# Results used one step later, and a ninth chain on GpSimd: one change to a four-stage convolutional network kernel

## The chip, the cores and the metric

The kernel is one launch on 1 core of one Trainium2 chip. The metric is the device time of that launch in microseconds, taken as the median of the runs shown. The core has five engines that each work through their own queue in order and meet only at semaphores: TensorE (PE; its weight loads are listed apart as PEld), VectorE (DVE), ScalarE (ACT), GpSimd (POOL) and SyncE (SP), which here only issues DMAs. An instruction that waits holds up everything behind it on its own engine.

## The reference, cut to what matters

Four images of 256 channels by 64 x 64 points pass through four layers, all in float32.

```python
# layer 0: 1x1 convolution, depthwise 3x3, offsets and masks; deformable sampling:
#   y = sum over 9 points of bilinear(image, grid + offset) * mask     (the gathers)
#   then the squeeze-and-excite scale and a feed-forward block
# layer 1: linear attention
#   qkv = relu(bn(w x));  agg = relu(pointwise(depthwise5x5(qkv)))     (the chains)
#   vk  = sum over points of v k^T;  out = (vk q) / (ksum q + eps);  x + relu(bn(w out))
# layer 2: 3x3 convolution with binarised weights, plus x
# layer 3: pooled attention: softmax(theta(x)^T phi(pool(x))) g(pool(x)), plus x
```

## The kernel before, in words

**Stages.** Images are handled one behind the other. `sample(n)` gathers image n (L554 to L674) while earlier images go through the later layers beside it. When the fourth image is gathered, the tail begins: `feedforward(3)`, then `layer1(3)` beside what is left of `layer2(2)` and `layer3(2)`, then `layer2(3)` beside the last rows of `layer3(2)`, then `layer3(3)` alone.

**How work is laid side by side.** Every layer is a generator. `beside` (L1183) advances the main one by a step, then advances each of the others until the costs they yielded reach their share. Inside `with ordered()` the instructions of PE, DVE, ACT and POOL stand in their queues exactly in the order in which the generators issue them; SP's order is left to a scheduler. So a `yield` is where other work may come in between, and whether it does depends on the costs. One round below is one step of `sample`: four gathers (`gathered`, L587) and eight matmuls on what they brought. Two rounds share a half of the PSUM tile `acc`, which ACT copies out at L603; after seven rounds the gather buffers `g` are used up, and a gather waits for PE.

**`layer3`, rows** (L1125 to L1158). For each of 32 rows of an image: two matmuls into `s`, DVE's maxima `mx` (L1138), ACT's exponentials `pe` (L1143), twice four transposes by PE (L1149) with a copy by ACT into `pT` (L1150), eight matmuls (L1154), DVE's reciprocal `rden` (L1156) and ACT's scaling into `m2` (L1157). A copy comes directly behind its transposes; L1154, L1156 and L1157 are issued without a yield between them.

**`layer1`.** `rows` makes 48 tiles of q, k and v (L805 to L815) into padded images `pad0` and `pad1`. Each of 24 chains is a depthwise 5 x 5 convolution of one padded image: on DVE it is 25 instructions over 1024 elements (taps, L178 and L180, in `depthwise`) that add up in the PSUM tile `agg`. In the tail (`alone` is true) every third chain goes aside: `products` (L186) makes 25 products on ACT (L193) and 24 additions on POOL (L194), one for every second tap of the two DVE chains beside it, and the next three chains begin when all are done. Everything else of the layer waits in the list `later`, from which `step` takes one item: `both` (transposes, the copy L853 and sums), `dens` (a matmul, DVE's L895 and the reciprocal L896), four times `head` (matmul L903, scaling L905) and twice `proj` (matmuls L911, ACT's L913, DVE's addition L914) for each half of an output block. In the tail a tap in two takes an item; what is left when the taps are done is worked off by L975.

**PSUM.** Eight banks: `agg` two, `acc`, `dp` and `vk` one each, and three under the tag `mm`, which all other results take in turn through `ps`. In the tail, the convolution's long sums take `acc` and `dp` instead.

Of the kernel before, what the change touches and what calls it, by code (L numbers as in the profile page):

```python
# [17 lines left out]
P = 128  # L18
# [23 lines left out]
LINEAR, LAST = 930, 620  # L42
# [29 lines left out]
class Net:  # L72
    def __init__(self, ctx, tc, a, out):
        self.tc, self.nc, self.a, self.out, self.kept = tc, tc.nc, a, out, []
        e = ctx.enter_context
        self.cp = e(tc.tile_pool(name="const", bufs=1, side="left"))
        self.ps1 = e(tc.tile_pool(name="ps1", bufs=1, space=PSUM))
        self.mm = e(tc.tile_pool(name="mm", bufs=3, space=PSUM))
        self.banks, self.alone = cycle(["mm"]), False
        self.dp = e(tc.tile_pool(name="scratch", bufs=1, space=DRAM))  # L80
# [105 lines left out]
    def products(self, pool, acc, src, w, k, rows, cols, r0, bias, step):  # L186

        nc = self.nc
        for t in range(k * k):
            s = src[:, r0 + t // k:r0 + t // k + rows, t % k:t % k + cols]  # L190
            if t:
                m = pool.tile([P, rows, cols], F32, name="m", tag="product", bufs=3)
                nc.scalar.activation(m, s, AF.Copy, scale=w[:, t:t + 1])  # L193
                nc.gpsimd.tensor_tensor(acc, acc, m, ALU.add)  # L194
            else:
                nc.scalar.activation(acc, s, AF.Identity, bias=bias, scale=w[:, t:t + 1])
# [551 lines left out]
    def layer1(self, n, st, st2):  # L748
# [3 lines left out]
        with tc.tile_pool(name=f"la{n}", bufs=1, side="right") as sp, \  # L752
# [14 lines left out]
            later, count, aside = [], 0, None  # L767
            room = lambda bufs, more=1: bufs + more * self.alone

            def step(cost, chains=False):  # L770


                nonlocal count
                count += chains
                if later and (not self.alone or count % 2 or not chains):
                    later.pop(0)()
                if chains:
                    if count % 8 == 6 if self.alone else count in LEADS:
                        next(made, None)
                    if count % 2 and aside:  # L780
                        next(aside, None)
                return cost

# [4 lines left out]
            def rows():  # L790


                for t, tiles in enumerate(((2, 4), (3, 5), (0, 1))):
                    new = lambda c: [self.padded(bp, 1, 20, 2, c, f"pad{i}", bufs=room(3, 2)) for i in range(2)]
                    pads = {0: new(0)}
                    for b in range(NB):
# [5 lines left out]
                        for i, m in enumerate(tiles):  # L802
                            ps = self.ps()
                            for k in range(KT):
                                nc.tensor.matmul(ps, qw[:, k, m * P:(m + 1) * P], x[:, k], start=k == 0, stop=k == KT - 1)  # L805
                            bn = {"bias": qb[:, m:m + 1], "scale": self.vec("qkv_s", m)}
# [14 lines left out]
                            yield  # L821
# [20 lines left out]
            def outer(t, kind, kv, vv, first, last):  # L842

                at = [slice(i, i + 256) for i in range(0, kv.shape[1], 256)]
                kts = []

                def turned(cs):
                    pt = self.ps("pt").rearrange("p (s j c) -> p s j c", s=2, j=2)
                    for j in range(2):
                        nc.tensor.transpose(pt[:, 0, j], kv[:, cs][:, j * P:(j + 1) * P], self.ident)  # L850
                        nc.tensor.transpose(pt[:, 1, j], vv[:, cs][:, j * P:(j + 1) * P], self.ident)
                    kts.append(bp.tile([P, 2, 2, P], F32, name="kt", tag="kt", bufs=4))
                    nc.scalar.copy(kts[-1], pt)  # L853
# [7 lines left out]
                def both(i):  # L861
                    if i < len(at):
                        turned(at[i])
                    if i:
                        added(i - 1)

                later.extend(partial(both, i) for i in range(len(at) + 1))
# [15 lines left out]
            def output(c, qp, aq):  # L883
# [3 lines left out]
                rd, xv, ot = [], [], {}  # L887

                def dens():
                    pd = self.ps("den")  # L890
                    for h in range(2):
                        for j in range(4):
                            nc.tensor.matmul(pd[32 * j:32 * j + 32], ld[:, j, h], qh[h][j], start=h == 0, stop=h == 1)
                    rd.append(bp.tile([P, 512], F32, name="rd", tag="v1"))
                    nc.vector.tensor_scalar(rd[0], pd, EPS_ATT, None, ALU.add)  # L895
                    nc.vector.reciprocal(rd[0], rd[0])  # L896

                def head(h, j):
                    if not j:
                        xv.append(self.block(bp, self.x3_d[n], 2 * c + h, "xq", bufs=1))  # L900
                    hs, i = slice(64 * (j // 2), 64 * (j // 2) + 64), 2 * h + j % 2
                    pb = self.ps("rden")
                    nc.tensor.matmul(pb, self.con("sel")[hs, i * P:(i + 1) * P], rd[0][hs], start=True, stop=True)  # L903
                    ot[h, j] = bp.tile([P, 512], F32, name="ot", tag="kt", bufs=4)
                    nc.vector.tensor_tensor(rw(ot[h, j]), qh[h][j], rw(pb), ALU.mult)  # L905

                def proj(h, m):
                    b, x = 2 * c + h, xv[h]
                    ps = self.ps()
                    for j in range(4):  # L910
                        nc.tensor.matmul(ps, pw[:, j, m * P:(m + 1) * P], ot[h, j], start=j == 0, stop=j == 3)  # L911
                    r = bp.tile([P, 512], F32, name="pr", tag="v0")
                    nc.scalar.activation(r, ps, AF.Relu, bias=self.vec("proj_b", m), scale=self.vec("proj_s", m))  # L913
                    nc.vector.tensor_tensor(x[:, m], x[:, m], r, ALU.add)  # L914
# [4 lines left out]
                later.append(dens)  # L919
                for h in range(2):  # L920
                    later.extend([partial(head, h, j) for j in range(4)] + [partial(proj, h, m) for m in range(KT)])
# [25 lines left out]
            if self.alone:  # L947
                for _ in range(8):
                    next(made)
                    yield step(1)  # L950
# [7 lines left out]

            while number < 6 * NCH:
                count = 0 if not self.alone and number % 2 == 0 else count  # L960
                *args, more = yield from chain()
                if self.alone:

                    *slow, smore = yield from chain()
                    aside = products(*slow, **smore)
                    yield from aggregate(*args, **more)
                    *args, more = yield from chain()
                    yield from aggregate(*args, **more)
# [363 lines left out]
```

## Time and profile before

| what | value |
|---|---|
| median of 3 runs | 7762.42 us (7758.1 to 7763.21) |
| the profiled execution | 7748.26 us, its span 7746.5 us |
| granted TensorE clock, mean | 0.839 |
| PE busy | 5899.6 us, 76% |
| DVE busy | 5126.8 us, 66% |
| POOL busy | 5035.0 us, 65% |
| ACT busy | 2148.7 us, 28% |
| gathers | first at 133.2 us, last at 6283.4 us |

Busy times are sums over the whole span. They do not tell which engine sets the pace of a stage, so the stages have to be looked at one by one. A row of a group of instructions reads: line, engine, operation, output and inputs, shapes and count, then busy time and mean duration in ns, then how long the engine stood idle directly before such instructions and what ended that. A row of the waits reads: waiting engine, its instruction, who released it, then the sum in us, the count and the longest.

### The profile page before, as it was taken

The page shows a single profiled execution, that of the slowest core. Times are in us where ns is not written, and L with a number is a line of the kernel's source. Part 1 is how long each engine was busy: PE and PEld are TensorE (multiplying, and loading weights), DVE is VectorE, ACT ScalarE, POOL GpSimd, SP SyncE. Part 2 cuts the span into 40 slices and gives each one's busy share as a digit, 9 for nine tenths or more (in the row PEclk, how much of TensorE's full clock was granted, in tenths as well). Part 3 has the DMA queues.
Part 4 walks back from the last instruction along what each step waited for, and adds up shares of the span by engine and source line. Part 5 has one row for each costly group of instructions (what it writes and reads, how often), then busy time and mean ns, then how long its engine had stood idle before and what let it go on. Part 6 is the DMA issues. An engine that isn't in the chain of part 4 may idle for free. (4 is left out here: it accounts for less than half of the span.)

```text
span 7746.5 us, 94023 instructions
## 1 busy us (share of the span) xinstructions
PE 5899.6 (76%) x35776; PEld 3468.2 (45%) x35776; DVE 5126.8 (66%) x6429; ACT 2148.7 (28%) x4623; POOL 5035.0 (65%) x4870
## 2 busy tenths in 40 slices
PE   5666666579676677888767778988677779977899
PEld 2333333334333333446545433466454434744487
DVE  6555553644788887239888883289888843999623
ACT  1111111112222211222233222222332222656415
POOL 2777777777777777767777667777776630866210
PEclk7676776779777677999888888999888889988999
DMA  6564664555544444555544445465444442211221
GB/s 188 152 178 137 171 173 140 164 182 157 159 123 124 128 139 135 167 151 160 150 137 132 118 149 161 139 171 159 137 132 123 120 132 65 75 52 36 76 81 52
DMA packets 744338, 1031.38 MB, mean 133 GB/s; under 512 B 354128, under 2 KB 459984, under 8 KB 742352
## 3 DMA queue, kind: packets, MB, share of 16 engines
q0 software_dynamic: 221184, 604.27, 27.0%
q1 hardware_dynamic: 522704, 421.10, 18.3%
q8 instruction: 283, 4.64, 0.3%
q14 instruction: 167, 1.37, 0.1%
HBM read 856.39 MB, written 168.61 MB: 132 GB/s over the span
## 5 line engine op out<-in xcount | busy, mean ns | idle before, releaser
L591 POOL DMA_INDIRECT g<-tab,sl x4608 | 4502.1, 977 | 1781.0 <-issue 1267.5
L178 DVE SCALAR_TENSOR_TENSOR agg<-pad,vec,agg 128x1024 f32<-128x1024 f32 x2280 | 2933.9, 1287 | 61.8
L598 PE MATMUL acc<-g,wm 128*32 128x128 f32 x18432 | 1288.4, 322 | 1248.4 <-ACT at L603 711.4
L598 PEld LDWEIGHTS acc<-g,wm 128*32 128x32 f32 x18432 | 631.2, 122 | 1955.1 <-ACT at L603 941.0
L1037 PE MATMUL ps<-xd,w 128*128 128x256 f32 x3072 | 711.4, 384 | 8.2 <-DVE x L1017 2.8
L582 DVE TENSOR_TENSOR wm<-con,sl 128x768 f32<-128x768 f32 x384 | 365.5, 953 | 412.6 <-PE acc L598 396.9
L1037 PEld LDWEIGHTS ps<-xd,w 128*128 128x128 f32 x3072 | 576.8, 192 | 108.2 <-issue 29.6
L618 ACT COPY dT<-dp 64x128 f32<-64x128 f32 x1152 | 295.7, 257 | 1117.2 <-PE dp L608 794.3
L730 PE MATMUL ps<-x2f,f 128*128 128x512 f32 x1024 | 479.1, 616 | 4.0 <-ACT f L705 4.0
L805 PE MATMUL ps<-xr,qw 128*128 128x512 f32 x768 | 454.4, 723 | 15.7 <-DVE ot L905 7.7
L740 PE MATMUL ps<-hm,f 128*128 128x512 f32 x1024 | 462.0, 600 | 0.0
L715 DVE SCALAR_TENSOR_TENSOR hm<-ps,vec,lk 128x512 f32<-128x512 f32 x256 | 192.1, 750 | 399.9 <-ACT lk L732 395.9
L988 POOL TENSOR_TENSOR xd<-xp 128x640 f32<-128x640 f32 x64 | 79.4, 1269 | 472.9 <-ACT xp L1000 280.9
L603 ACT COPY at<-acc 128x256 f32<-128x256 f32 x576 | 214.1, 372 | 488.6 <-PE acc L598 474.3
L732 ACT ACTIVATE lk<-ps,low 128x512 f32<-128x512 f32 x256 | 175.9, 687 | 595.5 <-PE ps L730 595.5
L608 PE MATMUL dp<-ident,at 128*128 128x128 f32 x1152 | 272.3, 324 | 73.2 <-ACT dT L618 61.2
L631 PE MATMUL po<-dT,ow 128*128 128x288 f32 x1024 | 307.6, 449 | 13.6 <-ACT dT L626 6.5
L1154 PEld LDWEIGHTS ps<-gt,pT 128*128 128x128 f32 x2048 | 289.6, 222 | 62.1 <-issue 40.3
L1154 PE MATMUL ps<-gt,pT 128*128 128x129 f32 x2048 | 303.6, 310 | 7.3 <-ACT pT L1150 6.9
L194 POOL TENSOR_TENSOR ak<-ak,m 128x1024 f32<-128x1024 f32 x96 | 227.2, 2366 | 114.1 <-ACT m L193 109.8
L730 PEld LDWEIGHTS ps<-x2f,f 128*128 128x128 f32 x1024 | 191.5, 195 | 230.0 <-issue 217.3
L1137 PE MATMUL s<-ph,th 128*128 128x512 f32 x512 | 274.2, 649 | 22.8 <-DVE r L1164 6.3
(243 smaller groups left out, 7395.8 us busy)
## 6 DMA issues: line engine op xcount, KB each, us to landing
g<-tab,sl POOLq DMA_INDIRECT x4608
x<-x SPq DMA_DIRECT2D x128, 512.0 KB
xr<-x SPq DMA_DIRECT2D x96, 512.0 KB
tab<-xo SPq DMA_DIRECT2D x192, 128.0 KB
x<-in_x SPq DMA_DIRECT2D x32, 512.0 KB
y<-yc SPq DMA_DIRECT2D x32, 512.0 KB
yb<-y SPq DMA_DIRECT2D x64, 256.0 KB
x<-yb SPq DMA_DIRECT2D x64, 256.0 KB
```

What stands on the lines that cost most here:

```text
L178: nc.vector.scalar_tensor_tensor(to, s, wt, acc, ALU.mult, ALU.add)
L582: nc.vector.tensor_tensor(wm, self.con("own").unsqueeze(1).unsqueeze(1).to_broadcast(sh), blocks[b][:, r:r + WR, G:].unsqueeze(3).to_broad ...
L591: nc.gpsimd.indirect_dma_start(out=g[:, i, :], out_offset=None, in_=table, in_offset=bass.IndirectOffsetOnAxis(ap=sl.bitcast(I32)[:, r, i: ...
L598: nc.tensor.matmul(acc[32 * i:32 * i + 32, :], wm[:, r4, 4 * i + 2 * x:4 * i + 2 * x + 2, :], g[:, i, x * P:(x + 1) * P], start=x == 0, st ...
L618: nc.scalar.copy(dT[b][hs, :, r:r + UR], dp[u][hs, :, :, s, :].rearrange("p v g o -> p g v o"))
L631: nc.tensor.matmul(po[m][:, 0:BR * OB], self.ow[:, k, m * P:(m + 1) * P], dT[b][:, k].rearrange("p r o -> p (r o)"), start=k == 0, stop=k ...
L730: nc.tensor.matmul(ps, f1[:, k, m * P:(m + 1) * P], x2[:, k], start=k == 0, stop=k == KT - 1)
L740: nc.tensor.matmul(ps, f2[:, k, m * P:(m + 1) * P], hm[:, k], start=k == 0, stop=k == 4 * KT - 1)
L805: nc.tensor.matmul(ps, qw[:, k, m * P:(m + 1) * P], x[:, k], start=k == 0, stop=k == KT - 1)
L1037: nc.tensor.matmul(ps[:, e], w[:, k, t, 2 * half + e, m * P:(m + 1) * P], v[:, 2 * half + e, k, t:t + 8], start=i % 6 == 0, stop=i % 6 == 5)
L1137: nc.tensor.matmul(s[i], tv[:, 4 * b + j], ph[:, i * 512:(i + 1) * 512], start=True, stop=True)
L1154: nc.tensor.matmul(ps[:, 0:P + 1], pT[:, m], gt[:, m], start=m == 0, stop=m == 7)
```

## The change

1. **`layer3`**: a yield stands between the four transposes and their copy, between the eight matmuls and `rden`, and between `rden` and `m2`. The costs of a row still add up to 9.5. While `spare` is set (the ordered part of the tail), `s` of the third image's rows goes to `acc` and `dp` instead of `mm`.
2. **`layer1` beside sampling**: the addition L914, with the statistics and the store that follow it, is issued an item later than its ACT instruction. `dens` and its reciprocal, and a head's matmul and its scaling, stay together.
3. **`layer1` in the tail**: every item is cut into stages (`staged`), and a stage is issued an item behind the one before. An output block is now 18 items instead of 13, with its heads and projections reordered; a key-value product of 256 points takes one item more. Half of the `rden` matmuls use the bank `vk`.
4. **The aside in the tail**: nine chains instead of eight, taken one after another from the same sequence and advanced by a fixed fraction at every tap, not in groups of three. POOL's addition is issued a step behind ACT's product. 15 chains stay on DVE.
5. **Buffers in the tail**: `kt`/`ot` 4 to 6, the projection's `xq` 1 to 2, `pad0` and `pad1` 5 to 4 each, the convolution's `xp` 1 to 2. A matmul of `rows` is one step ahead of its ACT instruction. The convolution's additions come three matmuls later. The cost of the layer is set to 592 from 620, that of a drained item to 2 from 4.

```diff
-LINEAR, LAST = 930, 620
+LINEAR, LAST, ASIDE = 930, 592, 9
...
     def products(self, pool, acc, src, w, k, rows, cols, r0, bias, step):
...
+        made = []
+        for t in range(k * k + 3):
+            if t < k * k:
+                s = src[:, r0 + t // k:r0 + t // k + rows, t % k:t % k + cols]
+                m = pool.tile([P, rows, cols], F32, name="m", tag="product", bufs=3) if t else acc
+                made.append(m)
+                if t:
+                    nc.scalar.activation(m, s, AF.Copy, scale=w[:, t:t + 1])
+                else:
+                    nc.scalar.activation(m, s, AF.Identity, bias=bias, scale=w[:, t:t + 1])
+            if 2 <= t <= k * k:
+                nc.gpsimd.tensor_tensor(acc, acc, made[t - 1], ALU.add)
             yield step(0.5)
...
-                    if count % 2 and aside:
-                        next(aside, None)
+                    if aside:
+                        due += ASIDE * 28 / (6 * NCH - ASIDE) / 25
+                        while due > 1:
+                            next(aside, None)
+                            due -= 1
...
+            def staged(items):
+                for i in range(len(items) + max(map(len, items)) - 1):
+                    now = [it[i - k] for k, it in enumerate(items) if 0 <= i - k < len(it)]
+                    later.append(lambda now=now: [f() for f in now])
...
+                if alone:
+                    staged([(partial(turned, cs), partial(copied, i), partial(added, i)) for i, cs in enumerate(at)])
...
+                if alone:
+                    order = [heads[0, j] for j in range(4)] + [heads[1, 0], outs[0, 0], heads[1, 1], outs[0, 1], heads[1, 2], heads[1, 3]]
+                    staged([(dens, inverse), none, none] + order + [none, outs[1, 0], outs[1, 1]])
+                else:
+                    joined = lambda *fs: [f() for f in fs]
+                    items = [(partial(joined, dens, inverse),)]
+                    for h in range(2):
+                        items += [(partial(joined, *heads[h, j]),) for j in range(4)]
+                        items += [(partial(joined, *outs[h, m][:2]), outs[h, m][2]) for m in range(KT)]
+                    staged(items)
...
+            def others():
+                for _ in range(ASIDE):
+                    while not (args := next(every)):
+                        yield
+                    *args, more = args
+                    yield from products(*args, **more)
...
             while later:
-                yield step(4)
+                yield step(2 if alone else 4)
...
-                    if not wide:
+                    if not wide and not self.spare:
                         s = [self.ps("s") for _ in range(2)]
...
                             nc.tensor.transpose(pt[:, m], pe[:, (4 * i + m) * P:(4 * i + m + 1) * P], self.ident)
+                        yield 1
                         nc.scalar.copy(pT[:, 4 * i:4 * i + 4], pt)
-                    yield 3
+                    yield 1
                     ps = self.ps()
                     for m in range(8):
                         nc.tensor.matmul(ps[:, 0:P + 1], pT[:, m], gt[:, m], start=m == 0, stop=m == 7)
+                    yield 1.5
                     rden = bp.tile([P, 1], F32, name="rden")
                     nc.vector.reciprocal(rden, ps[:, P:P + 1])
+                    yield 1.5
                     nc.scalar.activation(m2[:, j * P:(j + 1) * P], ps[:, 0:P], AF.Copy, scale=rden)
-                    yield 3
```

## The prediction, made before the changed kernel was run

> **What bounds the kernel now.** I read the windows first, to get the engines stage by stage, then the waits inside the stages that are not full, then a stretch of the timeline to see one wait pass through the queues.
>
> From 133 to 6283 us POOL gathers. Rows of the timeline show the pace: 0.95 us for a gather and 0.30 us of issue, 1.25 us in all, 5.0 us for a round of four. 4608 x 1.25 = 5760 us, but the stretch is 6150 us long. Of the rest, 298 us are gathers that waited for PE to give back a buffer (waits of POOL), 253 us of them after 3450 us, where rows of pooled attention run beside the gathers. The windows of the third image, and the waits in its second half:
>
> ```profile
> 3800.00:4200.00 400.00, 271.62 (x2160) 184.47 (x2152) 345.05 (x405) 135.55 (x319) 289.47 (x299) 0.84 0.47 138
> 4200.00:4620.00 420.00, 311.97 (x2039) 181.02 (x2038) 345.05 (x391) 119.60 (x272) 264.81 (x271) 0.84 0.44 132
> ...
> POOL g L591 <- PE acc L598: 84.3, 38, 11.2
> ...
> ACT m L1157 <- DVE rden L1156: 89.5, 18, 15.3
> ...
> DVE rden L1156 <- PE ps L1154: 23.6, 11, 7.7
> DVE xq L914 <- ACT pr L913: 16.9, 6, 5.4
> ```
>
> (A window's columns: its length, busy us with counts of PE, PEld, DVE, ACT and POOL, granted clock, DMA share, GB/s.) In the second window 271 gathers are 68 rounds, 339 us at POOL's pace, and DVE alone is busy 345 us. So DVE sets this stretch, and whatever it waits for is lost: 420 - 345 = 75 us are the most that better order can give here. In the first window DVE needs 345 us for 299 gathers (374 us) and has slack. How a DVE wait reaches POOL:
>
> ```profile
> 4477.76 0.17 DVE L1156 RECIPROCAL rden<-ps 128x1 f32<-128x1 f32 x1 [1.19 <-PE ps L1154]
> ...
> 4477.96 0.37 ACT L1157 ACTIVATE m<-ps,rden 128x128 f32<-128x128 f32 x1 [8.34 <-DVE rden L1156]
> ...
> 4479.76 1.08 PE L598 MATMUL acc<-g,wm 128*32 128x128 f32 x16 [2.04 <-ACT at L603]
> ...
> 4481.14 0.94 POOL L591 DMA_INDIRECT g<-tab,sl  x1 [4.76 <-PE acc L598]
> ```
>
> DVE waits 1.2 us for eight matmuls, ACT 8.3 us for DVE with the copy of `acc` behind it, PE for the copy, POOL for PE. The fourth image repeats this (stalls of 80.8 us between 5800 and 6200 us).
>
> The tail:
>
> ```profile
> 6575.00:6815.00 240.00, 227.67 (x1092) 184.80 (x1091) 230.56 (x263) 151.22 (x203) 204.06 (x99) 0.99 0.24 67
> 6815.00:7262.00 447.00, 322.59 (x1205) 194.26 (x1204) 413.86 (x484) 256.13 (x353) 281.19 (x119) 0.85 0.14 47
> 7262.00:7337.00 75.00, 69.81 (x277) 40.42 (x275) 29.80 (x50) 25.06 (x42) 0.00 (x0) 0.96 0.13 43
> 7360.00:7540.00 180.00, 175.40 (x828) 153.58 (x826) 53.03 (x118) 20.63 (x28) 37.88 (x31) 0.99 0.28 81
> ```
>
> First the last convolution rows of the third image, with PE and DVE at 95%; then DVE at 93%, alone; after the last tap (7262 us) the last output blocks, PE at 93%; then the fourth convolution, PE at 97%.
>
> **The change part by part.** Sums are against the profiled 7748.26 us; the median of the runs is 14.2 us above it, which I add at the end.
>
> *Rows beside the gathers (part 1).* A yield only helps if other work comes in between, so I counted rounds in the order of the built program. Of 64 rows, `rden` moves a round behind its matmuls in 34 and the scaling a round behind `rden` in 36; the rest stay in the same round. So about 0.53 of these waits should go. *L914 (part 2)* no longer stands in the round of its ACT instruction in 28 of 32 cases in these two images, 0.88. Where DVE sets the pace (4200 to 4620, 5800 to 6200 us) the waits are 23.6 + 20.9 for `rden` and 16.9 + 15.9 for L914: 0.53 x 44.5 + 0.88 x 32.8 = 52 us. In the two stretches before them `rden` waits 20.8 + 22.1 us, but DVE has slack there; I take a quarter of 0.53 x 42.9, 6 us. Together 58 us.
>
> What the yields add: the second copy into `pT` now falls into the round of L1154 in 54 of 64 rows (none before), so PE, with the next round's `acc` matmuls and transposes behind it, waits for ACT. The trace has no such wait of L1154. Nearest is PE's second group of transposes waiting for the first copy, 4.1 us in 6 cases, 0.7 us each; the other end is the mean of PE's waits for the copy of `acc`, 380.2 us in 167 cases, 2.3 us each, which is a copy that stands behind other ACT work. Below nothing it cannot go. I take 0.7, as it is the same copy behind the same kind of transposes: 38 us. Against it, PE's transposes wait for `pe` in the same round 16 times, not 32; half of the 46.7 us of that row, 23 us. Net 15 us. Sampling: -58 + 15 = **-43 us** (from -75 with no new wait to +65).
>
> The store that follows L914 is issued later on SP, and some loads of the next block's indices and of `xr` pass it. The only wait of a gather for its indices is the first one, 131.9 us at the start, so I cost this at nothing; the cover is the index load's lead of a block, 18 rounds or 90 us. If SP is blocked longer than that, POOL waits for the excess.
>
> *The ninth chain (part 4).* DVE loses 25 taps of 1.285 us, 32 us; ACT gains 25 x 1.16 = 29 us (57% busy, hidden) and POOL 24 x 2.366 = 57 us. Where it counts:
> - 6575 to 6815 us: 151 taps become 142. POOL needs 142 x 9 x 24 / 375 = 82 additions of 2.366 us and 32.4 us of the convolution's own: 226 us; PE still needs 228. DVE's 12 us are hidden under these two. 0 us (from -12, PE's floor, to +21, if POOL keeps its present 36 us of idling for ACT's products and becomes the bound).
> - 6815 to 7262 us: 246 taps become 231, 20 us off the binding engine. POOL's 133 additions are 314 us of some 405: covered.
>
> ```profile
> L914 DVE TENSOR_TENSOR xq<-xq,pr x16: 683/692/693, 7092.2 to 7335.9; 128x512 f32<-128x512 f32 x16
> ```
>
> A rule speaks against this part. The Trainium skill, "SBUF — State Buffer", section "Who interferes with whom", says that a DVE instruction with both inputs in SBUF and a GpSimd instruction that reads SBUF lock each other out for the whole instruction. L914 has both inputs in SBUF. By the rule it and L1099 (24 in the tail) would lose half an addition, 1.2 us, whenever POOL adds; with POOL's share up from 63 to about 78% that is 24 x 1.2 x 0.15 = 4 us more. By the row nothing is lost: minimum and maximum (683 to 693 ns) are 10 ns apart, though POOL adds beside most of them. I take 0.
>
> *Stages in the tail (part 3).* In the DVE-bound stretch DVE waits 10.3 us for L913 and 6.1 us for L1154; I take 10 of these 16. The output blocks' items, now 18 each against one item for two taps, fall behind: in the built order six more scalings, two more L914, two statistics and one inverse (4.1 + 1.4 + 1.3 + 4.0 = 11 us of DVE) come after the last tap. Stretch: -20 - 10 - 11 = -41 us (-30 to -50). The drain pays for it in PE time: six `rden` groups at 1.12, eight projection matmuls at 0.9, one `dens` at 3.1, and one attention row's 3.8 make 21 us; (69.8 + 21) / 0.98 = 93 us against 75: **+18 us** (+5 if it fills gaps, +35 if each of its 38 items pays a latency). Tail: 0 - 41 + 18 = **-23 us**.
>
> *Buffers (part 5).* With four pads, two or three edge memsets on DVE wait for the aside's last product on ACT, with the taps behind them; ACT is then at most two products of 1.16 us late. Up to 7 us, inside the range above. The rest only loosens waits that the rows show as small; the fourth convolution and the last attention are full of PE work and stay.
>
> Sum: -43 - 23 = **-66 us**: 7748.3 - 66 = 7682, in medians 7762.4 - 66 = **7696 us**.
>
> **The rivals** (medians).
> - *All listed waits go* and no new one comes: 0.53 x 87.4 + 0.88 x 32.8 = 75 us in sampling, tail -12 - 41 + 11 = -42: 7645 us. Against it: the order shows the new PE wait plainly.
> - *The next wait takes the place* in sampling: in the same stretches ACT waits 57.1 us for `mx`, which the change does not move, and a stall often has it as root. Only the tail is left: 7739 us.
> - *Slower: PE waits for the copies.* If the 54 copies come as late as the copies of `acc` do, 2.3 us, that is 123 us against 58 + 23 gained: 7804 us. It decides from (58 + 23) / 54 = 1.5 us a wait. For it: PE must serve a round in 5 us and its buffers are already used up there. Against it: ACT, freed of L1157's wait, reaches the copy sooner.
> - *The change does not do what it says:* 28 scalings and 30 reciprocals stay in their round; the factor 0.53 holds that.
>
> **How the numbers follow.** Forecast 0.50 (own range 7650 to 7750), all waits 0.10, tail only 0.20, slower 0.20. The range 7640 to 7775 us holds the first three and the near part of the fourth. 0.2%, about what a measurement here tells from no change, is 15.5 us: 7747 to 7778. Faster: 0.48 + 0.10 + 0.14 = 0.72; same: 0.02 + 0.06 + 0.02 = 0.10; slower 0.18.
>
> **What would show it.** The last gather some 40 us earlier; POOL's wait for PE after 3450 us down from 253 to about 210; DVE's waits for L1154 halved; a new PE wait for `pT` of about 38 us. In the tail 375 taps, the last one some 80 us earlier, and a drain of about 93 us. It is wrong if the new PE wait is over 80 us, if POOL's wait does not fall, or if POOL is full and DVE idle before the third convolution ends.

## The result and the profile after

The changed kernel takes **7761.0 us** (median; 7755.58 to 7769.89) beside 7763.82 us of the kernel before in the same session: ratio 0.9997, interval 0.9988 to 1.0006. No change; 7696 us, 66 less, had been forecast. A repetition (a_again, below) gave 0.9994 (0.9986 to 1.0003).

The profiled execution of the changed kernel took 7768.14 us, that of before 7748.26, so this pair alone would say +20 us. It says too much: the end of the gathers scatters between executions of one kernel (6276.6 and 6268.2 us in two profiles of the changed kernel). So the sampling is judged by timed runs, and the tail by its stages, which repeat within a few us. The windows of the changed kernel, stage by stage (last convolution rows of the third image; taps; drain, which is what the layer does behind its last tap; fourth convolution and last attention), and before them taps and drain of the kernel before, cut at the same instructions:

```profile
6820.30:7262.50 442.20, 317.79 (x1179) 190.75 (x1178) 409.17 (x480) 253.48 (x350) 276.46 (x118) 0.85 0.15 48
7262.50:7339.70 77.20, 70.75 (x279) 40.65 (x278) 30.33 (x53) 26.83 (x45) 0.00 (x0) 0.96 0.14 48
```

```profile
6543.00:6808.00 265.00, 253.61 (x1186) 201.38 (x1187) 226.33 (x282) 177.19 (x240) 235.07 (x115) 0.98 0.26 74
6808.00:7255.50 447.50, 314.46 (x1164) 193.78 (x1162) 406.29 (x454) 268.53 (x368) 318.28 (x134) 0.81 0.13 44
7255.50:7358.50 103.00, 90.78 (x316) 49.51 (x316) 43.01 (x70) 29.74 (x49) 0.00 (x0) 0.92 0.14 46
7358.50:7762.00 403.50, 382.05 (x1925) 309.01 (x1924) 137.52 (x320) 137.95 (x242) 39.54 (x32) 0.98 0.25 77
```

DVE is still busy 91% of the stretch of taps, with 25 taps fewer in the whole tail, and the stretch is no shorter. The drain, 77 us before, is 103: its PE work grew from 71 to 91 us and PE's share in it fell from 92 to 88%.

In the sampling the waits, third image, 4200 to 4620 us (released by whom, us, times, longest):

```profile
POOL g L595 <- PE acc L602: 66.1, 24, 7.1
...
ACT pT L1199 <- PE pt L1197: 45.8, 19, 11.0
...
ACT m L1208 <- DVE rden L1206: 42.5, 11, 8.5
...
DVE rden L1206 <- PE ps L1203: 18.0, 7, 8.6
```

Against 84.3, 19.5, 89.5 and 23.6 us before: ACT's wait for DVE is halved and POOL's falls by 18 us, while a wait that nobody had counted, ACT's for the transposes behind `pT`, more than doubles. The predicted new wait of PE for the copies is there. Over the whole kernel it is the last figure of this row of the page, 28.9 us; the waits from 3450 to 6284 us, which hold all 64 rows of the third and fourth image, show how much of it lies beside the gathers:

```profile
L1203 PE MATMUL ps<-gt,pT 128*128 128x129 f32 x2048 | 303.8, 308 | 29.4 <-ACT pT L1199 28.9
...
PE ps L1203 <- ACT pT L1199: 10.7, 12, 1.3
```

What had not been looked for is the duration of DVE's own instructions. Groups of DVE by form in the tail (6540 us to the end of the drain; count, then busy us and mean ns). First before:

```profile
L914 DVE TENSOR_TENSOR xq<-xq,pr 128x512 f32<-128x512 f32 x16 | 11.1, 691 | 33.4 <-ACT pr L913 33.4
...
L1102 DVE TENSOR_TENSOR xq<-m 128x256 f32<-128x256 f32 x8 | 7.5, 933 | 0.3
...
L1099 DVE TENSOR_TENSOR m<-x 128x512 f32<-128x512 f32 x8 | 6.6, 822 | 0.0
...
L878 DVE TENSOR_SCALAR ld<-con,kk 128x16 f32<-128x16 f32 x8 | 1.5, 231 | 0.1
```

and the same four groups in the changed kernel:

```profile
L1150 DVE TENSOR_TENSOR xq<-m 128x256 f32<-128x256 f32 x8 | 15.6, 1952 | 0.3
L949 DVE TENSOR_TENSOR xq<-xq,pr 128x512 f32<-128x512 f32 x16 | 14.7, 921 | 6.6 <-ACT pr L945 6.6
...
L1147 DVE TENSOR_TENSOR m<-x 128x512 f32<-128x512 f32 x8 | 10.3, 1289 | 0.0
...
L903 DVE TENSOR_SCALAR ld<-con,kk 128x16 f32<-128x16 f32 x8 | 8.7, 1135 | 0.1
```

The same instructions, the same shapes: 49.3 us in place of 26.7, **22.6 us more**, which is as much as the ninth chain takes off DVE in the stretch of taps (20 us by the prediction). They are the addition of an output block, the two maxima of layer3's pooling, and `ld`, a scaling of 16 columns by a number for each partition. Two timelines of the changed kernel show when it happens, DVE and then POOL (start, duration, both us; x3 is a run of three):

```profile
6847.26 2.46 DVE L1150 TENSOR_TENSOR xq<-m 128x256 f32<-128x256 f32 x1
6849.64 2.60 DVE L178 SCALAR_TENSOR_TENSOR agg<-pad,vec,agg 128x1024 f32<-128x1024 f32 x2
6852.15 0.69 DVE L1147 TENSOR_TENSOR m<-x 128x512 f32<-128x512 f32 x1
6852.88 2.46 DVE L1150 TENSOR_TENSOR xq<-m 128x256 f32<-128x256 f32 x1
```

```profile
6844.31 7.63 POOL L200 TENSOR_TENSOR av<-av,m 128x1024 f32<-128x1024 f32 x3 [0.22 <-ACT m L196]
6852.23 2.83 POOL L200 TENSOR_TENSOR av<-av,m 128x1024 f32<-128x1024 f32 x1 [0.28 <-ACT m L196]
```

A maximum over two SBUF operands that takes 0.42 us alone takes 2.46 us when an addition of 2.36 us runs on POOL, while the taps, with one operand in SBUF and the sum in PSUM, keep their 1.30 us beside it. Of the eight L1150 here six met an addition, and those six are the long ones. Nor are other DVE instructions longer beside POOL: up to the last tap 300 taps into `agg` that ran beside it took 1286 ns in the mean, and 45 that did not, 1286 as well. Of all groups of this stretch these four alone are longer by more than 0.1 us where they met POOL's work. This became the theory: **DVE and POOL lock each other out**, and the rivals: that POOL or ACT bounds the taps; that the long drain is the loss; that the yields cost what they gain.

### The profile page after: what moved, and what is told of

It is laid out like the page before. It is cut to its first block, busy times and chain, and to the rows that moved or that the text cites. A ratio compares the mean times of both kernels' runs of the same rounds, so it can differ in the third digit from the quotient of the medians.

```text
span 7766.4 us, 94114 instructions
## 1 busy us (share of the span) xinstructions
PE 5936.3 (76%) x35776; PEld 3485.1 (45%) x35776; DVE 5119.5 (66%) x6404; ACT 2170.7 (28%) x4648; POOL 5092.3 (66%) x4894
## 5 line engine op out<-in xcount | busy, mean ns | idle before, releaser
L178 DVE SCALAR_TENSOR_TENSOR agg<-pad,vec,agg 128x1024 f32<-128x1024 f32 x2257 | 2904.8, 1287 | 61.8
L586 DVE TENSOR_TENSOR wm<-con,sl 128x768 f32<-128x768 f32 x384 | 366.0, 954 | 417.2 <-PE acc L602 403.1
L200 POOL TENSOR_TENSOR av<-av,m 128x1024 f32<-128x1024 f32 x144 | 344.1, 2390 | 105.5 <-ACT m L196 96.8
L1203 PE MATMUL ps<-gt,pT 128*128 128x129 f32 x2048 | 303.8, 308 | 29.4 <-ACT pT L1199 28.9
L1203 PEld LDWEIGHTS ps<-gt,pT 128*128 128x128 f32 x2048 | 287.7, 220 | 74.2 <-ACT pT L1199 42.0
L744 PEld LDWEIGHTS ps<-hm,f 128*128 128x128 f32 x1024 | 188.6, 190 | 224.8 <-issue 221.7
```

Of the source, the lines that this page charges most:

```text
L178: nc.vector.scalar_tensor_tensor(to, s, wt, acc, ALU.mult, ALU.add)
L200: nc.gpsimd.tensor_tensor(acc, acc, made[t - 1], ALU.add)
L586: nc.vector.tensor_tensor(wm, self.con("own").unsqueeze(1).unsqueeze(1).to_broadcast(sh), blocks[b][:, r:r + WR, G:].unsqueeze(3).to_broad ...
L744: nc.tensor.matmul(ps, f2[:, k, m * P:(m + 1) * P], hm[:, k], start=k == 0, stop=k == 4 * KT - 1)
L1203: nc.tensor.matmul(ps[:, 0:P + 1], pT[:, m], gt[:, m], start=m == 0, stop=m == 7)
```

## The experiments

Fifteen runs in four sessions. In the first and the last session every kernel, that of before too (8774.04 and 8704.78 us, against 7762.79 and 7760.49 in the second and third), took about a millisecond more while the images are gathered: in b_yields POOL waits 558 us for what the profile calls "remote", of which the profile of before has none, and 638 us for PE, before 298. It is not the chip, though two of the expectations say so: the second and the last session ran on the same one. Ratios are therefore compared within a session; stages of the tail, which are alike, across sessions. Stages in us, from the profiles, cut at the first matmul of the last image's layer1, at the end of the third image's convolution (to 2 us), at the last tap and at the load of the fourth convolution's weights:

| kernel | session | ratio to before (interval) | conv. rows | taps | drain | rest |
|---|---|---|---|---|---|---|
| before | | 1 | 271.3 | 442.2 | 77.2 | 403.2 |
| changed | | 0.9997 (0.9988 to 1.0006) | 264.2 | 447.8 | 103.0 | 404.1 |
| b_yields | 1 | 1.0008 (0.9993 to 1.0024) | 271.2 | 454.1 | 75.9 | 407.5 |
| a_no_yields | 1 | 1.0028 (1.0018 to 1.0038) | 264.7 | 445.7 | 106.3 | 402.5 |
| a_port | 1 | 0.9979 (0.9967 to 0.9990) | 264.1 | 423.7 | 103.2 | 400.3 |
| a_drain | 1 | 1.0024 (1.0015 to 1.0033) | 264.3 | 470.0 | 74.4 | 418.0 |
| a_again | 2 | 0.9994 (0.9986 to 1.0003) | 265.2 | 447.5 | 103.0 | 403.1 |
| b_samp | 2 | 0.9970 (0.9957 to 0.9982) | 268.4 | 446.2 | 77.2 | 403.1 |
| a_all | 2 | 0.9974 (0.9965 to 0.9984) | 264.1 | 430.0 | 76.9 | 418.2 |
| a_ten | 2 | 1.0020 (1.0012 to 1.0028) | 283.7 | 420.6 | 121.5 | 404.7 |
| b_port | 3 | 1.0006 (0.9997 to 1.0015) | 271.4 | 443.8 | 79.2 | 403.4 |
| a_port2 | 3 | 0.9954 (0.9940 to 0.9968) | 264.2 | 420.6 | 103.2 | 399.9 |
| a_joined | 3 | 0.9976 (0.9967 to 0.9985) | 275.3 | 431.4 | 79.8 | 415.6 |
| b_late | 3 | 0.9991 (0.9982 to 1.0000) | 271.3 | 445.7 | 77.1 | 406.1 |
| a_pd | 4 | 0.9992 (0.9978 to 1.0006) | 261.9 | 455.6 | 79.4 | 403.1 |
| a_pd4 | 4 | 0.9982 (0.9968 to 0.9996) | 256.2 | 471.6 | 53.3 | 403.5 |
| a_pj | 4 | 1.0005 (0.9990 to 1.0021) | 265.0 | 459.7 | 81.7 | 400.7 |

Names that begin with b are edits of the kernel before, those with a of the changed one.

### The lock: a_port, b_port, a_port2

```diff
-nc.vector.tensor_scalar(ld[:, j, h, 16 * h:16 * h + 16], self.con("oh"), kk, None, ALU.mult)
+nc.scalar.activation(ld[:, j, h, 16 * h:16 * h + 16], self.con("oh"), AF.Copy, scale=kk)
-ps, pr[h, m] = pr[h, m], bp.tile([P, 512], F32, name="pr", tag="v0")
+ps = pr[h, m]
-nc.vector.tensor_tensor(m1, v[:, :, :, 0], v[:, :, :, 1], ALU.max)
+nc.vector.tensor_reduce(m1, v, AX.X, ALU.max)
```

The second maximum, into `xq`, becomes two such reductions, one for each half of the channels; the ReLU of a projection is then written in place, in PSUM. All of it in the ordered part of the tail alone. a_port2 is the kernel of a_port in the third session; b_port is the kernel before with these edits.

> The changed kernel with DVE's instructions that have two operands in SBUF taken out of the tail: the head's small scaling ld moves to ACT, the projection's ReLU is written in place into PSUM so that the addition xq <- xq + pr reads one operand from PSUM, and the two maxima of the pooling become reductions with one operand. The arithmetic is the same. Theory of the lock: beside POOL's streamed additions these four lost 23 us of DVE between 6540 and 7262 us; they should come back to the durations that they have beside no addition, ld leaves DVE (another 3 us), and the stretch from the end of the second convolution to the last tap becomes 15 to 23 us shorter: 7738 to 7746. Rival, that POOL or the waits between ACT and POOL set the stretch: durations fall, DVE idles more, and the time stays within 5 us of the changed kernel's 7761.

> The kernel before (eight chains in groups of three) with the same instructions taken off DVE's second SBUF operand in the tail. It tells whether these edits are good by themselves or undo something that the change brought. In the trace of before the excess of these instructions over their undisturbed durations is 8 us (the maxima alone; L914 and ld show none), and ld's 2 us leave DVE, so: at most 10 us less, 7753 to 7761, ratio 0.9987 to 1.000. Rival, that the edits help whatever POOL does: 20 us or more less, ratio 0.9975 or lower.

> The changed kernel without DVE's two-operand instructions in the tail, once more, on the chip of its comparison if it can be: before, on the chip with slow gathers, its taps' stretch was 424 us in place of 447.5. The same here makes 24 us less than the changed kernel's 7759.5: 7732 to 7740, ratio 0.996 to 0.9972.

Measured: taps 423.7 and 420.6 us in place of 447.5, 24 and 27 us less; a_port2 took 7728.07 us against 7760.49 of before, a gain of 32 us (25 to 47 by the interval of its ratio). The same edits on the kernel before give nothing (7766.74, ratio 1.0006). So they are not good in themselves: they undo what the change brought. The four edits were not tried one by one. DVE by form in a_port2 (the addition in its new form, then the second maximum), and its windows of taps and drain:

```profile
L954 DVE TENSOR_TENSOR xq<-xq,ps 128x512 f32<-128x512 f32 x16 | 10.8, 680 | 6.6 <-ACT ps L950 6.6
...
L1160 DVE TENSOR_REDUCE xq<-m 128x128 f32<-128x256 f32 x16 | 6.1, 421 | 0.3
```

```profile
6803.30:7223.90 420.60, 311.46 (x1166) 190.26 (x1165) 384.18 (x454) 270.07 (x376) 314.46 (x134) 0.83 0.14 47
7223.90:7327.10 103.20, 89.77 (x320) 48.86 (x316) 42.80 (x69) 29.63 (x49) 0.00 (x0) 0.93 0.13 46
```

Mean durations are the undisturbed ones again. DVE's busy time in the taps fell from 406.3 to 384.2 us with the same 454 records, and the stretch with it; DVE still idles 36 us. The rival (POOL or ACT sets the stretch) falls: POOL's busy time is all but unchanged (318.3 and 314.5 us), ACT's is not less, and the time went.

### The sampling alone: b_samp, b_late, b_yields, a_no_yields, a_again

b_samp has the sampling's part of the change without the tail's, b_late only L914 an item later, b_yields only the three yields (in the tail too), a_no_yields all but these.

```diff
 # b_late, b_samp, beside the sampling: the addition waits for the next item
-nc.vector.tensor_tensor(x[:, m], x[:, m], r, ALU.add)
+due.append(plus)
 # b_yields everywhere; b_samp only while images are gathered; a_no_yields takes them out
+yield 1      # before the copy into pT
+yield 1.5    # before rden, and again before the scaling
```

> The kernel before with the sampling's part of the change alone: the three yields in layer3's rows and L914 an item later, both only while the images are gathered; the tail issues what it issued before. The prediction's sum for this part was -43 us. From the profile of the changed kernel (last gather 8 us earlier, POOL's wait for PE 13 us less) I expect -5 to -12 us, a ratio of 0.9985 to 0.9994, with every stage of the tail as in the kernel before within 5 us. Rival: the waits that went are only replaced, ratio 1.000 within 0.0006.

> The kernel before with L914 an item later beside the sampling and nothing else; both parts of the sampling together measured -24 us. The prediction's terms were -29 us for this one (0.88 x 32.8) and -15 us for the yields (-30 + 15). If the waits for L913 are lost time as it took them, this is 20 to 29 us less, 7734 to 7743, and the yields are worth nothing. If the yields carry the gain, this is within 8 us of before. If it is shared, 10 to 15 us less.

> The kernel before with one thing added: the three yields in layer3's rows (transposes apart from their copy, matmuls from rden, rden from the scaling). Nothing in layer1 or in the aside is touched. The prediction's sum for this part alone: rden waits 0.53 x 44.5 + 6 = 30 us gained, new waits of PE 15 us lost, so -15 us, 7749. My theory now (the trace of the changed kernel has its last gather only 8 us earlier): the stalls are passed on to the next wait in the queues, and this is worth 0 to -8 us, 7756 to 7764; POOL's wait for PE after 3450 us falls by 10 to 20 of 253 us. Rival, that the yields do harm: PE's waits for the copies cost more than is gained, +5 to +15 us, 7769 to 7779, most of it in the tail, where rows of the third image run beside the convolution.

> The changed kernel with layer3's three yields taken out again; the addition used an item later, the staged tail, the ninth chain and the buffers stay. If the yields are worth what the sampling showed (8 us), the last gather is some 5 us later and the whole 0 to +8 us, 7761 to 7769. If in the tail the new waits (PE's L1203 for the copy 17 us, PE's L1212 for the scaling 17 us) cost real time, the tail is 10 to 15 us shorter than in the changed kernel and the whole -5 to -10 us, 7751 to 7756. If the prediction's part for sampling was right and only covered up by the tail, the last gather comes 15 us or more later, 7776.

> The changed kernel once more, unchanged, since the first experiments ran on a chip on which the gathers take a millisecond longer, and the changed kernel itself had not been timed there. By its first result 0.9997 of the kernel before. If the changed tail (longer by 20 to 27 us in every profile of it) is not made up by the sampling, which is far more disturbed on that chip, it is 1.001 to 1.004 there; on a chip like the first one 0.999 to 1.001.

b_samp: 7738.60 against 7762.79, **-24 us**, more than I then expected from one profile and outside both expectations. In the same session the changed kernel gave -3. So the sampling gains 24 us (14 to 33 by the interval) and the tail gives 21 of them back; by the stages of the two profiles the tail is 24 us longer (1485.1 against 1461.1 us from the last gather on). "No change" is a gain and a loss that happen to be equal.

b_late: 7752.90 against 7760.49, -8 us (0 to -14 by the interval); the rest, -16, is then the yields' (a difference of two ratios with intervals of about 0.001 each way, so good to some 12 us). Why so little comes of L914, in the waits of the whole of b_late:

```profile
POOL g L591 <- PE acc L598: 295.0, 176, 8.9
...
DVE rden L1173 <- PE ps L1171: 166.9, 78, 8.7
...
DVE xq L916 <- ACT pr L913: 72.5, 22, 9.3
```

and of before:

```profile
POOL g L591 <- PE acc L598: 297.7, 182, 11.2
...
DVE rden L1156 <- PE ps L1154: 148.2, 82, 7.7
DVE xq L914 <- ACT pr L913: 110.5, 39, 9.5
```

DVE waits 38 us less for L913, and 19 us more for the next matmuls in its queue; POOL, whose wait is the price, gets 3 us of it.

b_yields and a_no_yields ran in the session with slow gathers and without the changed kernel beside them, so of their times only this is used: the yields alone bring nothing there (1.0008). In the tail of before they lengthen the taps to 454 us (442 to 446 in the four profiles without them); in the changed tail taking them out changes 2 us. The rival that they cost what they gain in the changed tail is not borne out. The yields alone, beside the gathers and in a session like the second, were not run.

### The drain: a_drain, a_joined, a_all, a_pd, a_pd4, a_pj

```diff
 # a_drain (12), a_all (12), a_pd (12), a_pd4 (4)
-if later and (not alone or count % 2 or not chains):
+if later and (not alone or count % 2 or not chains or len(later) > 12):
 # a_joined, a_pj: no stages in the tail
-staged([(partial(turned, cs), partial(copied, i), partial(added, i)) ...])
+later.extend(partial(both, i) for i in range(len(at) + 1))
 # a_pd, a_pd4, a_pj: the cost that is used up
-LINEAR, LAST, ASIDE = 930, 592, 9
+LINEAR, LAST, ASIDE = 930, 570, 9     # 558 and 568 in the other two
```

All but a_drain have a_port's edits too; a_all also moves layer3's yields. An item here is one step of the layer's other work, as it stands in `later`; with the first edit one is taken at every tap while more than 12 (or 4) wait.

> The changed kernel with one condition added: an item of layer1 is also taken at a tap that has none, when more than 12 items are waiting. In the changed kernel 38 items were left after the last tap and the drain took 103 us, before 77. Theory that the drain is lost time which can be put beside the taps: the drain becomes 15 to 25 us shorter, the stretch of taps 5 to 12 us longer (the items' DVE work of 14 us moves into it), sum -8 to -15 us: 7746 to 7753. Rival, that it only moves: DVE sets the stretch, and each us taken from the drain is given back there, 7761 within 5 us.

> The changed kernel without the two-operand instructions and with the linear items of the tail put together again as they are beside the sampling (an output block 14 items, not 18; a product of 256 points one fewer), so about 166 items for the taps in place of 202. Theory that the staged items cost the drain's 26 us, and that nothing else of the tail depends on the staging: the drain (last tap to the load of the next weights) falls from 103 to 77 to 85 us, the stretch of taps rises from 424 by the 10 us of DVE work that comes back into it and by L914's waits, to 430 to 440: 8 to 14 us less than the last kernel, 7720 to 7732. Rival, that the stages hide waits which come back: the stretch is over 445 us and nothing is gained.

> The changed kernel with three edits: DVE's two-operand instructions out of the tail (measured alone: the stretch 24 us shorter), items taken at every tap when more than 12 wait (alone: drain 29 us shorter, stretch 22 us longer), and layer3's yields re-placed (both groups of transposes, then both copies, then the matmuls, rden and the scaling, each a yield apart, so that no instruction stands directly behind the one it needs). If the long drain's items cost the stretch so much because of the lock, the stretch with all three is about 430 us and the drain 75: 35 to 45 us less than the changed kernel. If they cost it their DVE time whatever the lock does, the stretch is 440 to 445 and the gain 24 to 30 us. If the yields' waits matter, the stretch is 5 to 10 us shorter still.

> As the changed kernel without two-operand instructions in the tail (7728 here, a drain of 103 us), and an item at every tap when more than 12 wait, with the cost of the layer set to what is then used up (570). In the two earlier kernels that shortened the drain to 77 to 80 us the layer ended with 3% of its cost unused, and rows of the third image were left to run alone, 12 to 15 us in the last stretch. With the cost mended: drain 77, the last stretch back at 400 to 403, the taps' stretch 430 to 436: 7716 to 7726 if the drain's time can be put beside taps. Rival: DVE sets the taps' stretch, every item put there is paid for in full there with its waits, and the time is 7728 or more.

> The same with more than 4 items waiting instead of 12 and a layer cost of 558; 21 items are left after the last tap, not 27 (38 in the changed kernel, 19 in the kernel before). If the drain's time can be put beside taps: drain 65 to 70, another 3 to 6 us less than with 12. Rival: no better, or worse, as the taps' stretch takes it all.

> The kernel with the linear items put together again, its layer cost mended in the same way (568 in place of 592). It measured 7742 with a last stretch of 416 us in place of 400. If the unused cost was the reason, 7726 to 7732, as good as the staged one: then staging the items brings nothing in the tail. If it stays at 7740 the stages are worth 12 us there, which the convolution's stretch (275 in place of 264 us) suggests.

a_drain: drain 29 us shorter, taps 22 us longer, and the last stretch 14 us longer. The last is a side effect: the layer then yields about 570 of its planned 592, `beside` goes on without it, and rows of the third image are left over; a_drain, a_joined and a_all show 1984 matmul records in the last stretch in place of 1925. So a_all (7741.93 us) and a_joined (7742.38) missed their expectations, though taps and drain came to 430 and 77, 431 and 80 us. With the cost mended (a_pd, a_pd4, a_pj) that stretch is back at 401 to 404, and nothing is won: from a_joined to a_pj, which differ in the cost alone, it is 15 us shorter and the convolution's 10, and the taps 28 us longer. The windows of taps and drain in a_pd4:

```profile
7771.60:8243.20 471.60, 345.99 (x1294) 207.18 (x1292) 410.57 (x491) 288.49 (x404) 324.19 (x138) 0.84 0.13 45
8243.20:8296.50 53.30, 49.19 (x187) 27.27 (x186) 25.65 (x43) 17.57 (x29) 0.00 (x0) 0.97 0.17 59
```

Drain and taps together: 524.9 us, 523.8 and 526.9 in a_port2 and a_port. Half the drain was put beside the taps, and the taps took 48 us more for it than in a_port, 26 us of it DVE's work and the rest new idling. **None of these orders won back the drain's 26 us**; the rival of a_drain and a_pd, that the taps' stretch takes what the drain gives, held; a_pd4 (0.9982) is no better than a_port (0.9979) in its own session. Without stages (a_pj) the two together are 541.4 us, against 535.0 with stages and as many items left (a_pd): the stages bring some 6 us, which the ratios of these two do not tell apart.

### One chain more: a_ten

```diff
-LINEAR, LAST, ASIDE = 930, 592, 9
+LINEAR, LAST, ASIDE = 930, 564, 10
```

> The changed kernel with DVE's two-operand instructions out of the tail, and ten chains aside in place of nine (cost of the layer 564 in place of 592). Theory that DVE is what bounds the stretch, and the aside is worth its 25 taps of 1.285 us once the lock is gone: 20 to 30 us less than the same with nine chains (stretch 424 us), so 395 to 405 us, while POOL is busy some 370 us of it. Rival, that POOL or ACT's products now bind: POOL needs 240 additions of 2.37 us = 569 us and the convolution's 61 us in 690, and waits for products 60 to 80 us already; then the stretch stays at 420 or grows, and DVE idles more.

With a_port's edits and ten chains aside: 7777.74 us, 15 us above before. Taps 420.6 as with nine, though DVE has 27 us less to do (356.8 us): it idles 64 us; the convolution's stretch, where POOL is busy 253 us, grows by 20, the drain by 18. With the lock gone, a tenth chain off DVE no longer shortens its stretch, as the rival had it; whether POOL or ACT's products hold it then was not found.

## Why the prediction was wrong

| step of the prediction | predicted | measured | from |
|---|---|---|---|
| L914's waits in sampling | -29 us | -8 | b_late |
| yields in sampling (-30 + 15) | -15 | -16, good to some 12 | b_samp less b_late |
| convolution's stretch | 0 (-12 to +21) | -6 to -7 | profiles |
| stretch of taps | -41 (-30 to -50) | +1 to +6 | profiles |
| drain | +18 (+5 to +35) | +26 | profiles |
| sum | -66 | about -3 | timed |

**The lock was taken at nothing.** This is the largest single failure, 24 to 27 of the 63 us that are missing, by a_port and a_port2. The prediction held the rule of the Trainium skill, "SBUF — State Buffer", section "Who interferes with whom", against the row of L914, "683/692/693", and argued: POOL adds beside most of these instructions, so the row shows no lock. The second half was never looked up, and it is false: laid over POOL's additions, **one of the 16** L914 of before meets an addition, and that one at its edge. In the changed kernel 8 of 16 meet one (one of them at its edge), all that start before the last addition ends. A row that never met the rival cannot speak against it. The evidence stood in two other rows of before: L1099, which the prediction set down by the rule but did not open, and L1102, which it left out, as it did `ld`. Their means are 822 and 933 ns where 684 and 425 are undisturbed; two of the eight L1102 took 2.45 and 2.46 us. And even by the rule the sum was 4 us, since it counted only the rise of POOL's share. That share rose (276 to 318 us of the taps' stretch), but what changed more is how often they meet: 4 of 8 L1099 before and 6 of 8 after, 3 and 6 of 8 L1102, none and all of the `ld`.

Why L914 met so few additions stands in the trace of before. ACT, POOL and DVE around the first:

```profile
7091.39 0.78 ACT L913 ACTIVATE pr<-ps,vec 128x512 f32<-128x512 f32 x1 [3.31 <-PE ps L911]
7092.07 1.16 ACT L193 ACTIVATE m<-pad,vec 128x1024 f32<-128x1024 f32 x1
...
7092.20 0.69 DVE L914 TENSOR_TENSOR xq<-xq,pr 128x512 f32<-128x512 f32 x1 [1.79 <-ACT pr L913]
...
7093.37 2.35 POOL L194 TENSOR_TENSOR av<-av,m 128x1024 f32<-128x1024 f32 x1 [3.74 <-ACT m L193]
```

ACT makes the product for POOL's next addition directly behind the ReLU that L914 waits for. L914 takes 0.69 us and the product 1.16, so L914 is done before the addition can start. It is the same at all ten L914 that stand between additions: POOL is waiting for ACT's product, and adds 0.3 to 0.5 us after L914 has ended. The old order, L914 right behind its ReLU, cost DVE a wait and kept the two apart; L914 an item later (part 3) and an addition a step behind its product (part 4) took that away. This is read from the trace; no run moved that order alone.

**The waits in the stretch of taps were taken as gone.** With the lock taken away the stretch is 420.6 to 423.7 us, 18 to 26 less than the 442 to 446 of before and its edits: about half of the -41. DVE's work in it fell from 409.2 to 384.2 us, 25 where 31 were counted; its idling, of which 10 us were to go, did not fall (33.0 us before, 36.4 in a_port2). Of the waits that it let go, that for L913 (10.3 us) did go and that for L1154 fell from 6.1 to 4.3 us, but in the same stretch of the changed kernel new ones came (7.6 us of `mx` for `s`, 0.8 before; 6.6 and 3.1 us at the output block's addition into `r`, none before).

**L914's waits were taken as lost time.** The step "where DVE sets the pace (4200 to 4620, 5800 to 6200 us) ..., whatever it waits for is lost" added up waits of one engine that follow one another; and by its own sum POOL needed 339 us of these 420 where DVE needed 345, so neither was full. The waits did go (in these two stretches 32.8 us fell to 3.8 in the changed kernel), but little came of it: in b_late the next wait, for the matmuls of `rden`, takes half of what was removed (19 of 38 us), the whole gains 8 us, and these rows do not show where the rest went. That is the second rival, "the next wait takes the place", for this half of the sampling; only, the next wait was another than the one it named.

**For the yields the number came out by luck.** -16 against -15 hides two terms that were off and cancel. In the stretches where DVE was to set the pace its waits for `rden` fell by 8.5 us (44.5 to 36.0), not by 24. The new wait of PE was put at 54 cases and 38 us; beside the gathers it is 12 cases and 10.7 us. PE's wait for `pe` fell by 17 us (46.7 to 29.7), where 23 were counted. And a large shift was in no sum: from 3450 to 6284 us ACT waits 130 us less for `rden` (266.6 to 136.8) and 61 us more for the transposes behind `pT` (62.2 to 123.3). No run tells what that one costs.

**The drain's mechanism was right and its size off**: 20 us more PE work, 21 predicted; but PE is busy 88% of it, not the 98% by which the prediction divided, though its own window showed 93%. It forecast 93 us, 103 came.

The slower rival (54 copies, 2.3 us late each) did not come: the 12 waits of L1203 beside the gathers are 0.9 us each, under its deciding point of 1.5. Of the signs, POOL's wait for PE after 3450 us fell from 253 to 231 us, not to 210, the last gather came 8 to 16 us earlier, not 40, and the last tap 7 to 15, not 80.

What stays open: without the lock, taps and drain together (523.8) are no shorter than before (519.4 to 523.4), although DVE has 12 us less work there (427.0 against 439.5 us). a_pd4 shows DVE idling 61 us in its taps, and no single wait of it is over 17 us. Which of them decides was not settled, and so 15 to 23 us of the -41 have no cause shown.

The version to keep is a_port2, the changed kernel with its DVE operands moved out of the way of POOL: 0.9954 (0.9940 to 0.9968) of the time before. In the first session, with the slow gathers, the same kernel gave 0.9979.

## What to carry to other kernels

Before moving elementwise work to GpSimd, list the DVE instructions that will run beside it, with where their operands lie. Here additions with an operand in PSUM and reductions lost nothing beside GpSimd's additions; two operands in SBUF, and the small scaling `ld`, lost up to about 2 us, most of an addition, each time they met one. Count the meetings, not GpSimd's share of the time. When a row is to show that something does not interfere, check first that the two ever overlapped. A wait can also be what keeps two instructions apart, so look at what runs behind it before it is removed. And a wait removed from an engine that works in order need not be worth its own length: here 38 us of waits were worth 8.

## What was not expected of the hardware

The length of the penalty: 0.42 us became 2.44 to 2.47 us in all six cases, longer than one addition's 2.36 us; why they are so alike is not shown. And a small instruction with one tensor operand and a scalar for each partition, `ld` with 128 x 16 elements, was hit nearly as hard as the large ones, from 231 to 1135 ns in the mean (four of eight took 1.98 to 2.23 us), while maxima as reductions (1213 ns for `m` in a_port2) and the taps were not. The same section of the Trainium skill's "SBUF — State Buffer", "Who interferes with whom", lists `tensor_scalar` among the forms that can take the pair shared with GpSimd and `tensor_reduce` among those that cannot, and the rows of `ld` and of the maxima agree. Not every scaling pays: L1187, one number a partition, took 214 ns alone and beside additions. POOL loses a little too: the three additions above took 7.63 us, three in a_port2 7.23.
